# Fourteen matrix products of a constant, placed ahead of the first edge search

## The chip, the cores and the metric

The kernel runs on one NeuronCore of a Trainium2 chip. The metric is the device time of one execution in microseconds (us), as a median over runs. All arithmetic is in 32-bit floats unless a line says otherwise.

## What is computed

The reference is one layer of a graph network over 3125 nodes with 256 features and 53,125 weighted edges. Cut to what matters:

```
xn  = layernorm(x)
h   = A @ xn                      # A: the weighted edges, summed by target node
gnn = tanh(mean over heads(...)) # two more products with A, softmaxes, small weights
mix = linear attention(xn)
x   = x + gnn + mix
out = x + mixture_of_experts(layernorm(x))   # 8 experts, one per row, capacity 489
```

The edges come sorted by target node. `A` is not given as a matrix: the kernel makes it, as a dense array of 3200 x 3200 floats in device memory (`adj`), from the lists of sources, targets and weights.

## The kernel before, in words

**Stages.** First the edges become `adj` (the function `from_runs`), while the rows of `x` are loaded and normalised and the first strip of `A @ xn` begins. Then TensorE forms the three products with `adj`, strip by strip, with the attention and the router set beside them. The experts come last.

**How `adj` is made.** Five nodes make a group; there are 625 groups. For each group the kernel takes 128 edges from the list, beginning at the first edge of the group, and a product of two selection matrices puts them into the group's five rows. Sixteen groups are a batch, so there are 40 batches (the last has one group). For each batch VectorE builds the selections (`cells` L617, `in_blk` L595, `in_row` L599 and L603, `lhs` L626), ScalarE widens one of them (`rhs` L639), TensorE multiplies (L654, four groups into one PSUM tile), ScalarE copies the result out (`st_rows` L658), and SyncE's queue stores about 1 MB into `adj` (L667, L668).

**How the first edge of each group is found.** This is the head of the kernel, and the place of the change.

1. The table of targets is loaded as 125 rows of 425 (`tab_i`, L444), in three transfers on SyncE's and ScalarE's queues.
2. VectorE compares the first targets of the rows with the group numbers (`part`, L471 and L474), and ScalarE converts the table to floats (`tab`, L467).
3. `search(c)` (L481), for 125 groups at a time: one product on TensorE picks the row of the table for each group (L484, 125 x 427), VectorE counts the targets in it that are below the group's first node (L487) and turns the count into an edge number (`start_i`, L492 and L493).
4. `gather(c)` (L506): GpSimd issues three indirect transfers that fetch sources, targets and weights at `start_i`.
5. TensorE turns the fetched blocks (`turn_some`, L538, transposes at L541), and the selections of batch 0 can begin.

Searches 0, 1 and 2 stand at the head (L558 to L566), with gathers 0 and 1 and the loads of `x` between them on GpSimd's queue. Searches 3 and 4 follow later, among the batches.

**What sets the order.** `from_runs` is written under a manual schedule: each engine executes its instructions in the order of the code. TensorE's order at the head is searches 0, 1, 2, then four transposes, then batch 0. PSUM tiles for the searches and the transposes come from `mm()` (L95), a pool of two that are handed out in turn. `ones` (L300, L301) is a constant of 128 x 128 that VectorE fills at the start.

Of the kernel before, what the change touches and what calls it, by code (L numbers as in the profile page):

```python
# [16 lines left out]
P = 128  # L17
# [57 lines left out]
def gps_layer(ctx: ExitStack, tc: tile.TileContext, a: dict, out: bass.AP):  # L75
    nc = tc.nc
# [16 lines left out]
    held = {}  # L93

    def mm():  # L95
        mm_pools.append(mm_pools.pop(0))
        return mm_pools[-1].tile([P, SW], FP, tag="mm", name="mm")
# [261 lines left out]
    def layer(net, runs):  # L359
# [67 lines left out]
        def from_runs():  # L427
# [49 lines left out]
            start = build.tile([GC, NC], FP)  # L477
# [77 lines left out]
                )  # L555

            early.close()
            fetched = []  # L558
            for c, piece in enumerate(X_PIECES):
                search(c)  # L560
# [139 lines left out]
            for b in range(last + 1):  # L700
# [21 lines left out]
                if turned:  # L722
                    q, _ = fetched[c]
# [32 lines left out]
        if runs:  # L756
            with tc.manual_schedule():
                sums = from_runs()
        else:
            general()  # L760
            load_w_kv()
            load_x(nc.scalar, 0, NT)
            for s in range(len(STRIPS)):
                norm_a(s)
                norm_b(s)
                norm_c(s)
                norm_d(s)
# [16 lines left out]
        if runs:  # L784
# [3 lines left out]
        w0T, w1T, b0, b1, gate_b, gate_c, gate_m, g_lo, ones = (  # L788
            held[x]
            for x in ("w0T", "w1T", "b0", "b1", "gate_b", "gate_c", "gate_m", "g_lo", "ones")  # L790
        )
# [915 lines left out]
```

## Time and profile before

| | us |
|---|---|
| median of three runs | 1012.25 |
| lowest and highest of the three | 1011.37 and 1013.17 |
| the profiled execution, device time | 1011.34 |
| its span in the trace | 1009.5 |
| TensorE busy | 977.7 (97%) |
| VectorE busy | 514.5 (51%) |
| ScalarE busy | 304.5 (30%) |
| GpSimd busy | 98.3 (10%) |

The span is what the trace covers; the device time of the same execution is 1.84 us longer. The shares are means over the whole span. The change touches only the first few microseconds, so the rows that matter are those of the head, which the prediction shows.

### The profile page before, as it was taken

How to read it: one execution, taken by the hardware profiler on the slowest of the kernel's cores; microseconds unless marked ns; L12 is line 12 of the kernel's file. 1: busy time of each engine (PE TensorE's matmuls, PEld its weight loads, DVE VectorE, ACT ScalarE, POOL GpSimd, SP SyncE). 2: the span in 40 equal slices, each digit the busy share in tenths (PEclk: the TensorE clock that was granted, in tenths of full speed). 3: DMA queues.
4: the chain of work that ended last, by engine and by line, in shares of the span. 5: the costliest groups of instructions: out<-in, count | busy, mean ns of one | idle time of the engine just before them, and what ended most of it. 6: DMA issues, size and time to landing. Idle time of an engine off the chain costs nothing.

```text
span 1009.5 us, 11457 instructions
## 1 busy us (share of the span) xinstructions
PE 977.7 (97%) x4202; PEld 635.9 (63%) x4202; DVE 514.5 (51%) x1149; ACT 304.5 (30%) x567; POOL 98.3 (10%) x113
## 2 busy tenths in 40 slices
PE   5889999999999999999999999999999999999996
PEld 3878888854444444455665554474444578888995
DVE  7999799800343444445653675575444465221211
ACT  3889889830000001001101001110111133224431
POOL 6511000000000000000000000000011142111111
PEclk7999999999999999999999999999999999999999
DMA  4989888993933247421475658769999797713300
GB/s 134 258 240 261 239 238 239 254 263 113 340 116 104 98 139 209 133 75 54 125 243 198 218 196 269 235 182 374 314 310 301 250 320 244 234 36 125 107 30 21
DMA packets 171641, 197.94 MB, mean 196 GB/s; under 512 B 7664, under 2 KB 118304, under 8 KB 171575
## 3 DMA queue, kind: packets, MB, share of 16 engines
q1 hardware_dynamic: 164285, 178.56, 56.6%
q0 software_dynamic: 7248, 18.51, 6.4%
q8 instruction: 35, 0.57, 0.2%
q14 instruction: 31, 0.25, 0.1%
q10 hardware_dynamic: 42, 0.05, 0.0%
HBM read 144.43 MB, written 53.37 MB: 196 GB/s over the span
## 4 chain that ended last, share of the span: by engine, by line
PE 85%; DMA 4%; DVE 4%; ACT 3%; issue 2%; SPq 1%; POOL 0%; POOLq 0%; ACTq 0%; DVEq 0%
PE acc L275 48%; PE mm L1205 7%; PE acc L1162 7%; PE acc L654 5%; PE b L654 5%; PE mm L833 4%; PE mm L889 2%; DMA adj<-st_rows 2%; PE pk L861 1%; ACT st_rows L658 1%; ACT rhs L639 1%; PE mm L916 1%; DMA at<-adj 1%; PE mm L1013 1%; PE mm L1306 1%
## 5 line engine op out<-in xcount | busy, mean ns | idle before, releaser
L275 PE MATMUL acc<-at,xn 128*128 128x512 f32 (+3 forms) x540 | 203.2, 523 | 1.3 <-DMA at<-adj 1.3
L275 PEld LDWEIGHTS acc<-at,xn 128*128 128x128 f32 (+1 forms) x540 | 96.4, 190 | 89.3 <-issue 75.1
L275 PE MATMUL acc<-at,g 128*128 128x512 f32 (+4 forms) x350 | 137.8, 541 | 0.0
L275 PE MATMUL acc<-at,late 128*128 128x512 f32 (+4 forms) x350 | 137.4, 543 | 0.0
L275 PEld LDWEIGHTS acc<-at,late 128*128 128x128 f32 (+1 forms) x350 | 62.4, 190 | 59.6 <-issue 54.1
L275 PEld LDWEIGHTS acc<-at,g 128*128 128x128 f32 (+1 forms) x350 | 62.9, 190 | 58.6 <-issue 52.3
L654 PE MATMUL acc<-rhs,lhs 128*125 128x128 f32 x626 | 85.7, 280 | 9.4 <-ACT rhs L639 8.5
L626 DVE TENSOR_TENSOR lhs<-in_row,in_blk 128x1000 f32<-128x1000 f32 (+1 forms) x79 | 90.3, 1183 | 1.2
L654 PEld LDWEIGHTS acc<-rhs,lhs 128*125 128x125 f32 x626 | 77.5, 191 | 20.9 <-ACT rhs L639 10.2
L654 PE MATMUL b<-rhs,lhs 128*125 128x128 f32 x624 | 81.9, 275 | 0.0
L654 PEld LDWEIGHTS b<-rhs,lhs 128*125 128x125 f32 x624 | 75.4, 190 | 0.0
L639 ACT CAST rhs<-cells 128x2048 f32<-128x2048 bf16 x39 | 74.9, 1920 | 0.2 <-DVE cells L617 0.2
L275 PE MATMUL acc<-a,xn 128*128 128x512 f32 (+1 forms) x160 | 73.1, 595 | 1.2 <-DMA a<-adj 1.1
L846 ACT ACTIVATE sq<-kv 128x512 f32<-128x512 f32 x25 | 15.8, 630 | 179.4 <-DVE kv L842 179.4
L1205 PE MATMUL mm<-w,hm 128*128 128x256 f32 (+2 forms) x288 | 64.3, 380 | 0.0
L839 DVE TENSOR_REDUCE kmean<-mm 128x8 f32<-128x512 f32 x25 | 17.3, 691 | 91.6 <-PE mm L833 91.6
L1162 PE MATMUL acc<-xeT,w 128*128 128x208 f32 (+2 forms) x288 | 58.9, 361 | 1.6 <-ACT hm L1166 0.9
L1205 PEld LDWEIGHTS mm<-w,hm 128*128 128x128 f32 (+2 forms) x288 | 51.2, 180 | 9.6
L1162 PEld LDWEIGHTS acc<-xeT,w 128*128 128x128 f32 x288 | 53.0, 190 | 5.7 <-ACT hm L1166 1.3
L658 ACT COPY st_rows<-acc 125x512 f32<-125x512 f32 (+1 forms) x79 | 47.6, 603 | 25.0 <-issue 14.5
L1166 ACT ACTIVATE hm<-acc,b_e 128x256 f32<-128x256 f32 (+2 forms) x72 | 32.4, 455 | 66.7 <-PE acc L1162 66.5
L617 DVE TENSOR_TENSOR cells<-steps_w,edge_h 128x2048 bf16<-128x2048 bf16 (+1 forms) x40 | 47.7, 1192 | 4.6 <-ACT rhs L639 4.4
(271 smaller groups left out, 1037.8 us busy)
## 6 DMA issues: line engine op xcount, KB each, us to landing
at<-adj SPq DMA_DIRECT2D x52, 1280.0 KB
adj<-st_rows SPq DMA_DIRECT2D x39, 896.0 KB
at<-adj SPq DMA_DIRECT2D x14, 1024.0 KB
at<-adj SPq DMA_DIRECT2D x12, 960.0 KB
w<-in_f_w SPq DMA_DIRECT2D x10, 1024.0 KB
a<-adj SPq DMA_DIRECT2D x39, 256.0 KB
at<-adj SPq DMA_DIRECT2D x12, 452.5 KB
adj<-st_rows SPq DMA_DIRECT2D x39, 104.0 KB
```

The source lines that it names most:

```text
L275: nc.tensor.matmul(ps[d][:, :w], stationary(c, d)[:k], a_rows[:k, :w], start=(c == 0), stop=(c == NT - 1),)
L617: nc.vector.tensor_tensor(cells[:, :m, :, :k], steps_w[:, None, :, :k].to_broadcast([P, m, P, k]), of_pairs(1, g0, ng, P), ALU.is_equal,)
L626: nc.vector.tensor_tensor(lhs[:, j::k], in_row[:, j::k, :, None].to_broadcast([P, m, GR, CA]), in_blk[:, :, None, :, j].to_broadcast([P, m ...
L639: nc.scalar.copy(rhs.rearrange("p (i j) c -> p i j c", j=2), cells.rearrange("p i c j -> p i j c"),)
L654: nc.tensor.matmul(p[:GP, j * P : (j + 1) * P], lhs[:, j0 + j], rhs[:, j0 + j], start=True, stop=True,)
L658: nc.scalar.copy(st[:GP, j0 : j0 + nj, :], p[:GP, : nj * P].rearrange("p (g b) -> p g b", b=P),)
L833: nc.tensor.matmul(pkv, xnT[:, d, t * P : (t + 1) * P], w_kv[:, d, :], start=(d == 0), stop=(d == 1),)
L839: nc.vector.tensor_reduce(mean, p3, AX.X, ALU.add)
L889: nc.tensor.matmul(p[:, j * D : (j + 1) * D], xnT[:, d, (t0 + j) * P : (t0 + j + 1) * P], w_mix[:, d, :], start=(d == 0), stop=(d == 1),)
L1162: nc.tensor.matmul(p[:, :slots], w1[:, d, f * P : (f + 1) * P], xeT[:, d, :slots], start=(d == 0), stop=(d == 1),)
L1166: nc.scalar.activation(hm[:, f, :slots], p[:, :slots], AF.Relu, bias=b1_e[:, f : f + 1], scale=1.0)
L1205: nc.tensor.matmul(p[:n, :D], hm[:, f, c : c + n], w2[:, f, :], start=(f == 0), stop=(f == FC - 1),)
```

## The change

One new PSUM tile is taken from `mm()`, and TensorE multiplies the constant `ones` (128 x 128) by itself fourteen times into it. Nothing reads the tile. In TensorE's order the products stand ahead of search 0. On all other engines the sequence of instructions stays what it was, and so does TensorE's behind the new ones; the only wait that is added is that of the first product for the filling of `ones`.

```diff
@@ -555,6 +555,10 @@
             early.close()
+
+            rise = mm()
+            for _ in range(14):
+                nc.tensor.matmul(rise[:, :P], held["ones"], held["ones"], start=True, stop=True)
             fetched = []
             for c, piece in enumerate(X_PIECES):
                 search(c)
```

## The prediction

> **What bounds the kernel now.** TensorE is busy for 977.7 of 1009.5 us, but the change lies where it is not: I read the chain of waits first, from 0 to 70 us, then the timeline of the head, then the granted clock there.
>
> ```profile
> 3.63 0.18 DVE ends_f L466
> ...
> 4.16 0.36 DVE part L474
> ...
> 4.65 1.77 PE mm L484 x2
> ...
> 6.45 0.68 DVE lt L487 x2
> ...
> 7.34 0.17 DVE start_i L493
> ...
> 7.82 1.41 POOL ends L512
> ...
> 11.07 3.52 DMA q<-in_edge_weight,start_i
> ...
> 16.09 2.32 DVE lhs L626 x2
> ...
> 18.46 1.64 PE acc L654 x6
> 20.10 1.71 PE b L654 x8
> 21.81 1.71 PE acc L654 x8
> ...
> 67.56 0.87 PE acc L654 x8
> ```
>
> Columns are start, length, engine, tile, line; "x8" counts records, two for each product. Until 18.5 us the chain is one long latency: table, compare, search 0, count, gather 0, transpose, selections, batch 0. Nothing runs beside it that could take its place. Search 0 is on it; searches 1 and 2 are not. The last three rows give a price: four products of 128 x 128 take 1.71 us at 20 us and 0.87 us at 67 us, so **0.4275 us a product slow and 0.2175 fast**.
>
> The same is seen in the clock (window, busy time and count, granted clock, DMA share, GB/s):
>
> ```profile
> 5.00:10.00 5.00, 4.26 (x6) 1.00 0.02 3
> 10.00:15.00 5.00, 1.22 (x4) 0.83 0.31 55
> 15.00:20.00 5.00, 2.40 (x10) 0.50 0.96 316
> 20.00:25.00 5.00, 5.00 (x32) 0.64 0.81 245
> 13.25:13.50 0.25, 0.06 (x1) 0.64 0.10 33
> 23.50:24.00 0.50, 0.50 (x7) 0.94 1.05 401
> ```
>
> The last two rows date a fall to half clock at 13.32 us (0.64 is 0.07 us at full and 0.18 at half) and a rise at 23.53. The 1.00 of the first row cannot be right: the three counts L487 start at 6.45, 7.87 and 9.30, each behind its search, so a search takes 1.42 us there, and its records have a median of 920 ns against a smallest of 519 when the same line runs after 39 us. **The searches run at half clock.** A transpose pair at 12.52 takes 0.41 us, a single one at 13.45 takes 0.44, so the clock had risen between 9.3 and 12.5.
>
> **When the clock moves.** Fall and rise are 10.21 us apart, three times 3.40. The Trainium skill (TensorE: Matmul & The Clock Gate, What's actually happening) says that a free-running window of 3.413 us decides: one busy window gives the full clock, one idle window takes it away. The trace agrees in period. Stepping back from 13.32 by 3.404 puts boundaries at 9.91, 6.51 and 3.11. Of the window 6.51 to 9.91 the searches fill 81% (4.61 us of records from 4.65, to 9.26) and the clock rose behind it; 16.72 to 20.13 has products for at most 71% and it didn't. So I take about 75% as enough, an estimate from these two windows.
>
> **The change part by part.**
>
> *Fourteen products.* They can start when `ones` is filled:
>
> ```profile
> 1.20 0.17 DVE L301 MEMSET ones<- 128x128 f32 x1
> ```
>
> That ends at 1.37; the first search started 0.14 us after the compare it waited for (4.52 to 4.65), so they start at 1.5. The window to 6.51 is then full and the clock rises there: 5.0 us at half clock are 11.7 products, the other 2.3 take 0.5 us, and the fourteen end at **7.0 us**. The table and compare that they were to fill are over at 4.6. Had they run at full clock, 14 x 0.2175 = 3.05 us would have ended at 4.55, just in time; but the clock begins low. Their weight loads cost nothing of their own: the prices above contain them, as each L654 product has one.
>
> *The searches.* They now run at full clock, 0.71 us instead of 1.42. Search 0 ends at 7.0 + 0.71 = 7.7 instead of 4.65 + 1.42 = 6.07: **1.65 us late**. Search 2 ends at 9.15 instead of 8.9, and is not on the chain.
>
> *Here the skill's rule is weighed.* The same page (Why this matters for your kernels) advises to warm up with at least 4 us of products, which speaks for the change: search 0 would gain 0.71 us. But it also says there that gaps over about 3 us between bursts lose the clock, and the trace shows that one: behind the searches TensorE has only four transposes until 17.5. By the advice the change is worth -0.7; by the row (start 1.5, half clock until 6.5, gap behind) it is +1.65. I take the row: fourteen products at the slow price last 6.0 us, and only 3.1 us are free.
>
> *Bounds of the delay.* I can't know the window's phase in another execution. Earliest rise: 75% of a window after 1.5, at 4.05; 6.0 products are done, 8.0 more take 1.74, search 0 ends at 6.5, **+0.4**. Latest: at 7.5 all fourteen are through at half clock and search 0 ends near 8.2, **+2.2**. If the clock never rises for them, 7.5 + 1.42 = 8.9, +2.8.
>
> *What is queued behind.* Search 0 holds VectorE's L487, then `start_i`; GpSimd's three gathers and, behind them on its queue, the first load of `x` (12.29) and gather 1. All of that is late alike. SyncE's queue has nothing until the first store at 25.12; its own order is untouched. The PSUM turn moves by one tile: search 1 now follows the fill in its tile instead of search 0, and is in order on the same engine, so there is no new wait.
>
> *What of the delay is given back.* Batch 0 would start at 18.46 + 1.65 = 20.1. If the rise stays at 23.53, it then has 8.0 products done at half clock instead of 11.9, and the remaining 7 of 15 take 1.5 us: it ends at 25.05 instead of 24.2, only 0.8 late. But VectorE and ScalarE carry the full delay: the `lhs` of batch 1 is done at 23.4 + 1.65 = 25.1, and VectorE is busy 4.9 of each 5 us from 20 to 40. DMA is between 0.81 and 1.08 busy from 15 to 40, with `x` starting later by the whole delay. So between 0.8 and 1.65 goes on; I take 1.5, near the full value, as three of four resources carry it.
>
> *Behind that* nothing can take it back: from 57.7 us on TensorE sets the chain nearly without a hole, and later waits (the turn at 217 to 222 us, a load at 250) follow from the work ahead of them. **Sum: +1.5 us**, on the profiled execution 1011.34 + 1.5 = 1012.8. The median shown is 0.9 above that execution, so the forecast for it is **1013.8 us**, +0.15%. About 0.2%, 2.0 us, is what a measurement of this kernel can tell from no change; the forecast is just inside.
>
> **The rivals.**
>
> *The clock slips by a window at batch 0.* The shifted start, 20.1, lies on the boundary at 20.13. A little later, or at another phase, and the window to 23.53 is not full: the rise comes at 26.9. Then 3.4 us at half clock cost 1.7 more: +3.2, **1015.5**. For it: the margin is almost nothing. Against it: 75% would be enough, and then 20.98 is the limit. Chance 18%.
>
> *The fill doesn't raise the clock*, since a constant may not count as activity, or the searches' window begins anew. Search 0 ends at 8.9: +2.8, **1015.1**. No row shows such products. Chance 10%.
>
> *The delay is hidden.* Batch 0's regained 0.8 us, and the DMA backlog that bounds 25 to 44 us (the chain has two stores of 7.9 and 9.4 us there), swallow it: +0.3, **1012.6**. Against it: the backlog itself begins later. Chance 14%.
>
> *Faster: the clock, once up, stays up until batch 0.* TensorE is busy for 7.6 us before the gap instead of 4.6; if the gate weighs a longer past, no fall comes at 13.3. With the smallest delay (+0.4) batch 0 starts at 18.9 and its 15 products take 3.3 us: done at 22.2 instead of 24.2, -2.0; VectorE's `lhs` for batch 1 at 23.8 allows -0.5 at first, and -2.0 only if the stores, not VectorE, set what follows. It decides in its favour where a full-clock batch 0 gains more than search 0 loses, a delay under about 2 us. Up to -2.0: **1010.3**. Against it: the fall came 4.1 us after search 2, with two transposes in that stretch. Chance 10%.
>
> **How the numbers follow.** The forecast has 48%. Its own range is +0.4 to +2.2 with half a microsecond of scatter in the runs; four tenths of it lie over +2.0. Slower by over 0.2%: 0.19 from it, 0.17 and 0.09 from the first two rivals: 0.45. Faster by over 0.2%: the last rival's upper part and scatter, 0.08. Within: 0.47. The range leaves out most of the faster rival and the far end of the clock's slip: 1011.7 to 1016.0.
>
> **What would show it.** Right: fourteen products from 1.5 us, the pace falling from 0.43 to 0.22 within them; search records near 520 ns; the first `start_i` near 9.0 instead of 7.34; gather 0, the first store and the first strip late by about the same. Search records at 920 ns speak for the second rival; a rise of the clock near 27 us for the first; no half clock at 15 to 20 us for the last. The prediction is wrong if search 0 ends before 6.1, or if the delay at the first store is not found again at 220 us.

## The result and the profile after

| | before | changed |
|---|---|---|
| median of 20 runs, us | 1011.91 | 1015.02 |
| lowest and highest | 1009.51 and 1013.67 | 1012.77 and 1018.54 |
| ratio to before (95% interval) | | 1.0030 (1.0021 to 1.0039) |
| span of the profiled execution | 1009.5 | 1013.6 |

The change makes the kernel slower by 3.1 us here. Two more comparisons, told of below, gave ratios of 1.0015 and 1.0018; weighted by the width of their intervals the three give 1.0022, with about 0.0006 to either side, or +2.2 us; the first lies further from the second than their intervals make likely, so this mean is a rough one. The profiled execution lost 4.1 us of span, more than a typical one.

The chain of waits of the changed kernel (start, length, engine, tile, line) shows the same sequence as before with one new link:

```profile
1.42 6.28 PE mm L561 x28
7.70 0.73 PE mm L484 x2
...
9.34 0.17 DVE start_i L493
...
13.07 3.51 DMA q<-in_edge_weight,start_i
...
18.08 2.32 DVE lhs L630 x2
...
20.45 1.64 PE acc L658 x6
```

Search 0 no longer waits for the table but for the fourteen products: they are still running at 7.5 us, and the compare was ready at 4.5, as in before. Everything behind is late by 2.0 us: `start_i` 9.34 against 7.34, `lhs` 18.08 against 16.09, the first products of batch 0 20.45 against 18.46.

The answers for the two lines on TensorE (count, then shortest, median and longest record in ns, first and last start):

```profile
L561 PE MATMUL mm<-ones x28: 358/421/582, 1.4 to 7.3; 128*128 128x128 f32 x28
L484 PE MATMUL mm<-tab,part x10: 519/522/594, 7.5 to 56.2; 125*125 125x427 f32 x10
```

The searches did get the full clock: a median record of 522 ns, where those at the head of before had 920. The products paid for it. Their own records overlap (28 with a median of 421 ns lie within 6.28 us), so the pace is read from the whole: fourteen products in 6.28 us are 0.45 us each, the half-clock price almost to the end.

The granted clock (window, busy time and count, clock, DMA share, GB/s) dates a fall in the gap behind the searches at 14.33 us, a rise in batch 0 at 24.57, and a second stretch at half clock, from 45.1 to 51.9, that the first trace of before doesn't have:

```profile
14.00:14.50 0.50, 0.00 (x0) 0.83 0.02 4
24.50:25.00 0.50, 0.50 (x6) 0.93 0.65 139
45.00:50.00 5.00, 4.28 (x20) 0.51 1.08 311
50.00:55.00 5.00, 5.00 (x39) 0.81 1.01 298
```

Ahead of that second stretch the stores of `adj` come late. SyncE's queue, the fourth store of before and then of the changed kernel:

```profile
38.77 0.83 SPq L667 DMA_DIRECT2D adj<-st_rows  x1
```

```profile
42.93 0.80 SPq L671 DMA_DIRECT2D adj<-st_rows  x1
```

The first store is 1.5 us late (26.63 against 25.12), the fourth 4.2, and the ninth, where the build is past this stretch, 5.0 (67.91 against 62.93). So this one execution has two losses: 2.0 us at the head, and more in the stretch between 30 and 45 us. There the DMA share is 0.87 to 1.09, ScalarE waits for stores, and one store on the chain took 12.00 us, where the two on that of before took 7.86 and 9.39. Which of the two losses belongs to the change, the experiments had to tell.

### The profile page after: what moved, and what is told of

Same layout as the page of the kernel before. It is cut to its first block, busy times and chain, and to the rows that moved or that the text cites. A ratio compares the mean times of both kernels' runs of the same rounds, so it can differ in the third digit from the quotient of the medians.

```text
span 1013.6 us, 11514 instructions
## 1 busy us (share of the span) xinstructions
PE 984.3 (97%) x4230; PEld 643.8 (64%) x4230; DVE 514.3 (51%) x1149; ACT 305.0 (30%) x567; POOL 99.3 (10%) x113
## 4 chain that ended last, share of the span: by engine, by line
PE 86%; DVE 4%; DMA 4%; ACT 3%; issue 2%; SPq 1%; POOL 0%; POOLq 0%; ACTq 0%; DVEq 0%
PE acc L275 47%; PE mm L1209 7%; PE acc L1166 7%; PE acc L658 6%; PE b L658 5%; PE mm L837 4%; PE mm L893 2%; DMA at<-adj 1%; PE pk L865 1%; DMA adj<-st_rows 1%; ACT rhs L643 1%; ACT st_rows L662 1%; PE mm L920 1%; PE mm L561 1%; PE mm L1310 1%
```

## The experiments

Each kernel was compared with runs of before on its own chip. The medians of before differed from chip to chip (1011.6 to 1013.1 us), so only ratios are compared across the groups; the experiments of one group share their runs of before. A ratio of 0.001 is 1.0 us.

### The changed kernel twice more

No edit.

> The changed kernel once more, for a second trace and more times. Theory H (the head): the late search 0 shifts the head by 2.0 us (start_i at 9.34 against 7.34, to 0.7 us by the phase of the clock), the first store comes near 26.6 instead of 25.1, and the median is +2 to +4 on before. Rival C (the clock): what exceeds the head's delay comes from a second fall of the clock near 45 us; then this trace, too, shows a fall between 40 and 55 us whenever its span is 3 or more above that of before, and none where it is about 2 above. Rival D (DMA): the excess comes from stores that land late behind other transfers between 28 and 44 us (the wait for a store that ended at 43.3); then it is there with or without the fall.

> The changed kernel a third time, since the two comparisons so far gave 1.0030 and 1.0015. Theory H: start_i is late by what the phase of the clock gives, 0.7 to 2.0 us (8.0 for a rise of the clock near 4.7 us, 9.3 for one near 7.5), mean about 1.3, and the ratio lies near 1.0015 to 1.0025. If the middle adds to it systematically, 1.003 again.

Measured: 1.0015 (1.0006 to 1.0025) and 1.0018 (1.0004 to 1.0032). The two timelines of TensorE, first the second trace, then the third:

```profile
1.42 4.95 PE L561 MATMUL mm<-ones 128*128 128x128 f32 x28 [1.42 <-DVE run L800]
```

```profile
1.42 5.21 PE L561 MATMUL mm<-ones 128*128 128x128 f32 x28 [1.42 <-DVE run L800]
```

The same fourteen products took 6.28, 4.95 and 5.21 us, and `start_i` came at 9.34, 8.01 and 8.28. The fall of the clock came at 14.33, 11.54 and 12.10 in these traces; fall and rise of the first trace are 10.24 us apart, three windows of 3.41, and two windows ahead of the falls are 7.5, 4.7 and 5.3 us. With half pace up to there and full pace behind it, the fourteen end at 7.5, 6.1 and 6.4 us, and `start_i` follows 1.84 us later in the first: that makes 7.9 and 8.2 for the other two. The delay of the head is thus a matter of the phase of the clock's window, as theory H has it, and the phase differs from one execution to the next.

The second trace also shows a second fall of the clock (49.1 to 52.5 us, span 1011.7), the third none (span 1010.3). For the spans of 2.2 and 0.8 us above the first trace of before, rival C had asked for a fall only from 3 up: it missed in the second trace.

### Seven products

```diff
-            for _ in range(14):
+            for _ in range(7):
```

> Seven products instead of fourteen. They end near 1.42 + 3.0 = 4.4 us, ahead of the compare (4.52), so search 0 starts at 4.65 as before. Theory H: no delay; start_i at 7.3 or, where the clock has risen by then, up to 0.7 earlier; median 0 to -1 on before. A rival that puts the loss on the products themselves (a used PSUM tile, instructions to fetch, the clock's later state) expects half of the loss, +1 to +2, to stay.

```profile
1.41 3.36 PE L561 MATMUL mm<-ones 128*128 128x128 f32 x14 [1.41 <-DVE run L800]
4.71 1.02 PE L484 MATMUL mm<-tab,part 125*125 125x427 f32 x2
```

Seven do fit ahead of the compare. Search 0 starts where it always did, and the clock rose during it: it took 1.02 us, between the 0.73 behind fourteen products and the 1.77 of before. `start_i` came at 6.66, 0.7 earlier than before. The ratio is 1.0007 (0.9998 to 1.0017). No loss is shown, but the hoped-for gain isn't there either: 0.7 us less would be 0.9993, outside the interval. The rival's "half of the loss" (+1 to +2) is not excluded by this run alone, and the interval overlaps that of fourteen products on the same chip (1.0006 to 1.0025). A price for each product, about 0.15 us, would fit seven, fourteen and twenty-eight as well as the delay does; what speaks against it are the thirty products put into the gaps, below: at that price they would cost 4.5 us, and no loss shows.

### The delay without the products

```diff
             part = seek.tile([EL, NG], FP)
+            idle = find.tile([P, NG], FP)
+            for _ in range(4):
+                nc.vector.tensor_copy(idle, ti)
```

(in the kernel before, no products)

> No products: VectorE copies a table of no use four times ahead of the compare, about 2.0 us, so search 0 starts near 6.65, at half clock, and start_i comes near 9.3 as in the changed kernel. Theory H: the whole loss is there without the products, +2 to +4, as in the changed kernel. The rival that puts the loss on the products: +0 to +1.

```profile
9.20 0.15 DVE L496 TENSOR_SCALAR start_i<-start 125x1 int32<-125x1 f32 x1
```

Measured: `start_i` at 9.20, ratio 1.0019 (1.0010 to 1.0028), +1.9 us for a head 1.86 us late. TensorE does nothing extra here, and its searches run at half clock. A delay alone brings a loss of its own size; the rival's +1 is at the edge of the interval.

### Twice the products

```diff
-            for _ in range(14):
+            for _ in range(28):
```

> Twenty-eight products. The first fourteen end near 7.5, the others at full clock in 3.05 us; search 0 starts near 10.6 and start_i comes near 12.4, 5.1 late. Theory H: +5 to +7 on before, the median rising with the delay of start_i by 1.0 to 1.4 us per us. If the build of the adjacency matrix took delays in (hidden behind DMA), less than +3.5.

```profile
11.98 0.15 DVE L493 TENSOR_SCALAR start_i<-start 125x1 int32<-125x1 f32 x1
```

Measured: `start_i` at 11.98, 4.64 late, and a ratio of 1.0042 (1.0029 to 1.0055), +4.2 us. Six runs stand behind it. The expected +5 to +7 was too high, though its lower end lies in the interval; the measured loss is about 0.9 us per us of delay. That the build took in a larger part of it (less than +3.5) is not what was measured, though the interval begins below that.

### The kernel before, once more

> The kernel before, once more, for a second trace. In the traces so far the loss against the first trace of before is there by 65 us, and is the shift of the first store (-1.2 to +4.0) plus 1.8 to 3.0 us, with a second fall of the clock between 42 and 52 us in all of them and none in that of before. Theory H2: the second fall belongs to both kernels and the first trace of before is a lucky one; this trace shows a fall between 40 and 66 us or, without one, a span near 1009.5; the change costs only its shift of the first store. Rival M (the middle): the change causes the fall; this trace shows none, as the first.

Measured: 0.9996 (0.9984 to 1.0007), as it has to be, and a trace with a second fall:

```profile
45.00:50.00 5.00, 3.40 (x18) 0.71 1.01 285
50.00:55.00 5.00, 5.00 (x41) 0.95 0.94 255
```

Its span is 1009.4, that of the first trace 1009.5. So the second fall belongs to both kernels, against rival M, and in this pair it cost nothing that the span shows. Nor did it make the excess in the traces of the changed kernel: the first was 4.2 us late at its fourth store, at 42.93, before its clock fell at 45.1, and only 0.8 us came on top up to the ninth. The second was 3.6 us late at its fifth store (47.84 against 44.24), before its fall at 49.1, and 3.2 at the ninth. That disposes of rival C. In both, the excess came between the first and the fifth store.

### Taking the DMA collision away

GpSimd's ten loads of constants (0.5 to 128 KB each, issued between 27.9 and 36.2 us in before) fall together with the first stores. They are moved in both kernels:

```diff
-            for load in loads:
-                load()
...
+                if b == 16:
+                    for load in loads:
+                        load()
                 if b == 24:
                     load_w_kv()
```

> The kernel before, with GpSimd's ten loads of constants issued at batch 16 instead of ahead of batch 0. Rival D (DMA collision): the stores of batches 1 to 4 no longer wait behind them; the wait of ScalarE for a store between 33 and 44 us goes, the fifth store comes near 43 or earlier, there is no second fall of the clock, and the time falls by 1 to 3 us. If the constants are not the cause: the same within 1 us.

> The changed kernel with the same loads issued at batch 16. Rival D: the collision is gone here as well, so what is left of the change is the shift at the head, +0.5 to +2 us on the kernel with late constants and no change; the fifth store follows the first by 19 us or less instead of 21.8. If the head's shift alone makes the loss: +2 to +3 as between the two kernels without this edit, and the time near that of the changed kernel.

Measured: 1.0022 (1.0012 to 1.0033) without the products and 1.0041 (1.0029 to 1.0054) with them. SyncE's queue, first with late constants and no products, then in the kernel before; the 1st, 6th, 9th and 17th store:

```profile
24.82 0.33 SPq L667 DMA_DIRECT2D adj<-st_rows  x1
...
45.64 0.66 SPq L667 DMA_DIRECT2D adj<-st_rows  x1
...
62.97 0.30 SPq L667 DMA_DIRECT2D adj<-st_rows  x1
...
109.00 0.95 SPq L667 DMA_DIRECT2D adj<-st_rows  x1
```

```profile
25.12 0.33 SPq L667 DMA_DIRECT2D adj<-st_rows  x1
...
48.20 1.21 SPq L667 DMA_DIRECT2D adj<-st_rows  x1
...
62.93 0.80 SPq L667 DMA_DIRECT2D adj<-st_rows  x1
...
104.23 1.05 SPq L667 DMA_DIRECT2D adj<-st_rows  x1
```

Half of rival D is right: the fifth store came at 41.54, as forecast, and the sixth 2.6 us earlier than in before. But by the ninth nothing is left of that, and the time, which D had falling by 1 to 3 us, rose by 2.2. Where the constants are issued now, from 81 us on, the build falls behind, by 4.8 us at the seventeenth store; why it loses more there is not shown. The second fall of the clock is there too (47.1 to 50.5 us), which D had excluded. For the question at hand the pair says this: with the collision taken away from the head, the products still cost 1.0041/1.0022 = 1.0019, or 1.9 us, with about 1.3 us to either side by the scatter of the runs, and VectorE's `lhs` of batch 1 is 1.8 us late (22.64 against 20.86). So the loss is there without this collision.

### Batch 0 late, searches and loads on time

```diff
+            for _ in range(6):
+                nc.vector.tensor_copy(lt, tab[:GC, :EK])
             prepare(0)
             widen(0)
```

(in the kernel before, no products; `lt` is a scratch tile)

> No products. Search 0, the gathers and the loads of x run as before (start_i at 7.3), but VectorE makes six copies of no use ahead of the selections of batch 0, so that batch 0 and the first store come 1.5 to 2.4 us later. Theory X (the start of the DMA work carries): the stores' backlog takes the delay in, the fourth store comes near 39 as before, +0 to +1 us. Theory S (the first store carries): +1.5 to +2.4.

```profile
12.84 2.81 DVE L685 COPY lt<-tab 125x425 f32<-125x425 f32 x6
17.52 2.31 DVE L626 TENSOR_TENSOR lhs<-in_row,in_blk 128x1000 f32<-128x1000 f32 x2
22.68 2.31 DVE L626 TENSOR_TENSOR lhs<-in_row,in_blk 128x1000 f32<-128x1000 f32 x2
25.83 0.33 SPq L667 DMA_DIRECT2D adj<-st_rows  x1
```

Measured: 1.0016 (1.0003 to 1.0029). `start_i` was on time at 7.17, the first store 0.7 to 0.9 late, VectorE's `lhs` 1.4 (batch 0) and 1.6 (batch 1). The loss of 1.6 us is of the size of what VectorE lost. Theory X expected the fourth store near 39, and it came at 39.40; its 0 to +1 us is not refuted by the interval, but misses the value. S had +1.5 to +2.4 for a first store 1.5 to 2.4 late, which it was not.

### Products in the gaps

Seven products ahead of search 0, fourteen between search 2 and the transposes, nine ahead of batch 0, run twice; and a version with eight and eight in the two later places alone:

```diff
+            rise = mm()
+            for _ in range(7):
+                nc.tensor.matmul(rise[:, :P], held["ones"], held["ones"], start=True, stop=True)
             fetched = []
...
             search(2)
+            rise = mm()
+            for _ in range(14):
+                nc.tensor.matmul(rise[:, :P], held["ones"], held["ones"], start=True, stop=True)
             turn_ends(0, *fetched[0])
             turn_some(0, fetched[0][0], edge_h, 1, 2)
             turn_some(0, fetched[0][0], edge, 0, 3)
+            rise = mm()
+            for _ in range(9):
+                nc.tensor.matmul(rise[:, :P], held["ones"], held["ones"], start=True, stop=True)
```

> Seven products ahead of search 0, fourteen between search 2 and the transposes, nine between the transposes and batch 0: all in TensorE's free time. Theory of the gap: the clock, risen by 6 to 8 us, does not fall before batch 0, whose fifteen products then take 3.3 us instead of 5.8; the first store comes near 22 to 23 us instead of 25.1. If the first store sets what follows: -1 to -3 us on before. If the middle takes it back: 0 to -1.

> The kernel with seven, fourteen and nine products once more; its first comparison gave 0.9992 (0.9984 to 1.0000). Theory X: start_i comes 0.6 us earlier, so about -0.6 (0.9994). Theory S: the first store came 2.5 us earlier, -2.5 (0.9975).

> No products ahead of search 0; eight between search 2 and the transposes and eight ahead of batch 0, to hold the clock. start_i stays at 7.3; where the clock holds, batch 0 runs at full speed and the first store comes at 23 to 23.7 instead of 25.0. Theory X: 0 to -0.5 us. Theory S: -1.5 to -2.

Measured: 0.9992 (0.9984 to 1.0000) and 1.0004 (0.9989 to 1.0019); the version without the seven 1.0011 (0.9999 to 1.0024). With thirty products the clock did hold: the nine ahead of batch 0 took 2.18 us both times, the full-clock pace. With eight and eight it did not. It fell at 14.2 us, the eight ahead of batch 0 took 3.44 us, and it rose again at 17.6, just as batch 0 began. In all three batch 0 ran at full speed, and the first store came at 22.54, 22.79 and 23.11 us, 2 to 2.6 earlier than in before. Nothing comes of it: no version is shown to beat the kernel before. Theory S, by which the whole head start of the first store would be gained, lies outside all three intervals. The timeline of the version with eight and eight shows why at the head, beside the `lhs` of batch 1 in before:

```profile
14.52 3.44 PE L572 MATMUL mm<-ones 128*128 128x128 f32 x16
...
15.71 2.36 DVE L632 TENSOR_TENSOR lhs<-in_row,in_blk 128x1000 f32<-128x1000 f32 x2
...
19.76 1.04 PE L660 MATMUL acc<-rhs,lhs 128*125 128x128 f32 x8
20.64 1.04 PE L660 MATMUL b<-rhs,lhs 128*125 128x128 f32 x8
20.80 2.31 DVE L632 TENSOR_TENSOR lhs<-in_row,in_blk 128x1000 f32<-128x1000 f32 x2
...
23.17 0.92 PE L660 MATMUL acc<-rhs,lhs 128*125 128x128 f32 x6 [0.56 <-DVE lhs L632]
```

```profile
21.12 2.31 DVE L626 TENSOR_TENSOR lhs<-in_row,in_blk 128x1000 f32<-128x1000 f32 x2
```

TensorE is through with batch 0 at 21.7 instead of 24.5, and then waits, in the end for VectorE, whose `lhs` of batch 1 comes at 20.80, 0.3 earlier than in before. At the head of the build VectorE goes its own pace: the `lhs` of batches 0, 1 and 2 start 5.0 to 5.2 and 3.4 us apart in every trace, whatever TensorE's clock. What is left of the head start is gone in the stretch of the stores: with seven, fourteen and nine the first store was 2.6 us early, the second 1.8, and the fourth not at all (38.79).

### What fits all of them

Neither X nor S, as written down ahead, fits every run. A third reading, formed after the runs, does better: what counts is when VectorE's selections start. The start of `lhs` of batch 1 in the one trace of a kernel, against 21.12 in before, beside the loss measured over all of its runs:

| kernel | `lhs` of batch 1, us | loss, us |
|---|---|---|
| 28 products | +4.6 | +4.2 |
| delay on VectorE ahead of search 0 | +1.8 | +1.9 |
| late constants, with against without products | +1.8 | +1.9 |
| batch 0 late | +1.6 | +1.6 |
| 14 products, three traces and comparisons | +2.0, +0.5, +0.6 | +3.0, +1.5, +1.8 |
| 8 and 8 products behind the searches | -0.3 | +1.1 (-0.1 to +2.4) |
| 7, 14 and 9 products, twice | -0.9, -0.6 | -0.8, +0.4 |
| 7 products | -0.7 | +0.7 (-0.2 to +1.7) |

In the first four rows the late start is carried nearly one to one, within intervals of about 1 us to either side. The changed kernel's own second and third trace, +0.5 and +0.6 beside +1.5 and +1.8, don't fit that well. That the reading was found afterwards is a reason for care, and an earlier start isn't shown to gain: of four attempts one gained 0.8 us at the edge of its interval and three showed no gain.

Inside a single execution the tie is loose. From the `lhs` of batch 1 to the ninth store, measured against the first trace of before, the other traces lost up to 3.4 us more or took back up to 0.3; the second trace of before itself lost 0.8 there. So the stretch of the stores adds from one execution to the next as much as the change costs. What decides how much it adds is not shown.

## Why the prediction was right or wrong

**Right in kind.** The fourteen began at 1.42 (forecast 1.5), the first of them at half clock, and ended behind the compare. The searches got the full clock. The clock fell in the gap behind them, at 14.3 us, and batch 0 was slow again up to 24.6. "By the row" was right against the advice to warm up: where the products themselves run slow, fourteen last up to 6 us and only 3.1 are free.

**The end of the fourteen** was put at 7.0 us and search 0 at 1.65 late, from a rise of the clock at 6.5. In the trace it rose near 7.5 and `start_i` was 2.0 late. The window's grid was right, its phase can't be carried from one execution to another: four traces with fourteen products gave delays of 0.7, 0.9, 1.5 and 2.0 us (the third is the one with late constants), all within the bounds of +0.4 to +2.2.

**The forecast of +1.5 us** was too low against the +3.1 measured first, and a little below the +2.2 (1.6 to 2.8) of three comparisons. Two terms of the sum had about the right size. The delay of the head was put at 1.65 us; it was 2.0 in the first trace and 1.2 in the mean of three. Of it I let 1.5 go on, 0.91 us per us; twenty-eight products gave 0.9, and the delay alone cost 1.9 us for 1.86. My reason for taking a little off, the 0.8 us that batch 0 regains, was a poor one. The regained time is real, even more than I put: the first store of two of the traces came at 24.48 and 24.84, earlier than in before. But no run shows it to be worth anything.

What the sum has no term for is the stretch from 25 to 65 us, which I let hand the delay on unchanged, or swallow it in one rival. In the three traces of the changed kernel the first store was 1.5 us late, 0.6 early and 0.3 early; the ninth was 5.0, 3.2 and 0.4 late. With a mean head delay of 1.2 us, handed on one to one, about 1 us of the +2.2 stays without a cause. It may arise in that stretch, or the delays of the runs without a trace may have been larger; one trace for each comparison is too few to say. So the direction and the head were foreseen, but that the first +3.1 still fell into the range owes something to luck: the forecast's own bounds end at +2.2, and the rest of the range was there for scatter and for rivals that did not come true.

**The rivals.** The clock did not slip by a window at batch 0 in the trace of after; it rose at 24.6, early enough. A second fall came 20 us later, but before has it as well. The fill does raise the clock. The delay was not hidden. And the clock did not stay up through the gap, until thirty products in all were put around the searches; then it did, but the gain I gave that rival with "-2.0 only if the stores, not VectorE, set what follows" failed at just that condition.

**"The prediction is wrong if ... the delay at the first store is not found again at 220 us."** It was a poor test: the first store was 1.5 us late, 0.6 early or 0.3 early, the last one, at 219.15 in before, 4.9 late, 3.3 late and 0.1 early, and all three comparisons showed a loss.

## What to carry to other kernels

Work that is to raise TensorE's clock must be paid at the low clock, and ends when its pace at that clock lets it: size it by that (here seven products, not fourteen, and even seven showed no gain), and look for the gap behind it in which the clock falls again. The latency chain at the start of this kernel passed a forced delay on nearly in full, but TensorE made faster in it gained nothing that shows: VectorE set the pace of the next stage, and the stores that of the one behind it. And two traces of the same kernel before an explanation of a few microseconds: the stretch at half clock that stood out in the single pair turned out to belong to both.

## What the hardware showed beyond that

The clock's record is blind at its beginning: it reads 1.00 until its first fall, while the searches of before and the fourteen products run at half pace. In the run with batch 0 late it reads 1.00 throughout the head, although four products there take 1.71 us (21.32 to 23.03) and 0.87 soon after (24.15 to 25.02). Only the pace of like instructions tells.

Products of a constant with itself raise the clock: behind fourteen of them the searches' records had a median of 522 ns instead of 920, and behind seven the clock rose during search 0.

A half-filled stretch did not keep the clock. In the version with eight and eight it fell at 14.2 us, although in the 3.41 us before that TensorE had products for 1.05 us and transposes for 0.71.
